# Layer 0's columns behind an up scan: their loads on GpSimd's queue instead of ScalarE's

## The chip, the cores and the metric

The kernel runs on one core of one Trainium2 chip. The metric is the device time of one execution in microseconds (us); lower is better. A core has a matrix engine (TensorE, PE in the profile; PEld is its weight load), a vector engine (VectorE, DVE), a scalar engine (ScalarE, ACT), a general engine (GpSimd, POOL) and SyncE (SP), which only issues DMA transfers. ScalarE and GpSimd can issue transfers as well. Each engine works through its own instructions in order, and all transfers are carried out by the core's 16 DMA engines.

## The reference

The input x has the shape (32, 48, 64, 128): batch, channels, height, width. Two layers are computed, each as x = x + scan(groupnorm(x)). A scan goes over the image four times: down and up over the 64 rows, with one set of weights, then right and left over the 128 columns. Each step adds a convolution of the row (or column) before it, with five taps along the row (or column) and 48 x 48 channels:

```python
def step(w, b):
    def f(carry, inp):
        nxt = inp + _conv1d(carry, w, b)
        return (nxt, nxt)
    return f
...
_, d_rest = jax.lax.scan(step(down_w, down_b), d0, xs[1:])
...
_, u_rest = jax.lax.scan(step(down_w, down_b), u0, seq)
...
_, r_rest = jax.lax.scan(step(right_w, right_b), r0, ws[1:])
...
_, l_rest = jax.lax.scan(step(left_w, left_b), l0, R[Ww - 2::-1])
...
x = x + _L0_conv_ref(_gn(x), L0_conv_down_w, ...)
x = x + _L1_conv_ref(_gn(x), L1_conv_down_w, ...)
```

So a column scan can't begin before the up scan of the same images has ended: column 0 holds an element of every row.

## The kernel before

The batch is cut into four groups of 8 images. `PHASES` (line 75) lists the work in the order in which TensorE does it: a "rows" phase is the down and up scan of one group (126 steps), a "cols" phase is the right and left scan of a pair of groups (254 steps). For layer 0 the order is rows of groups 0 and 1, columns of pair 0, rows of group 2, rows of group 0 of layer 1, rows of group 3, columns of pair 1. Each of the two column phases of layer 0 thus follows directly on the rows of its pair's second group; `follows` (line 800) is true for these two phases alone.

A step (`step`, line 647) makes nine matrix products, three for each third of the 384 channel places, and a VectorE add (L667) for each third, which takes the product from PSUM and one tensor from SBUF. Three large slots of the `arena` hold the rows or columns that are worked on.

Rows and columns have different layouts in SBUF, and the data goes from one to the other by way of a DRAM tensor, `upa` for layer 0. `move_rows` (line 517) stores rows of the up scan there as they are finished; with `to_dram` it makes ten transfers for eight rows, one for each entry of `PIECES`. `load_unit` (line 561) loads columns from there, also in up to ten transfers for one run over the three thirds. The 128 columns are taken in four quarters j of 32; a quarter has six units i, a third (o) of one group of the pair (half). Units with half = 1 belong to the group whose up scan has just ended. Within a unit `a` counts eight runs of eight rows (a = 0 is rows 0-7), and `e` is the row inside the run. All transfers go through `dma` (L199), which uses SyncE's queue if it isn't given another.

When something is issued is written out by hand. `at(t, ...)` (line 737) puts a call on an agenda, t in scan steps; `catch_up` (line 1072) makes the calls that are due before each step, and `in_order` (line 203) keeps the instructions of each engine in that order. t0 is the step at which a phase begins. The last rows of an up scan are stored at these times: the cut [2, 8) when row 2 is done, the cut [0, 2) at the end (`plan_rows`, line 770). `plan_cols` (line 805) loads quarter 0 of the group just scanned in five calls that follow the stores: runs 4-7, 2-3, 1, then rows 2-7, then rows 0-1. Quarter 1 comes at t0 + 1.5, quarter 2 from t0 + 8.

```python
at(t0 + 1.5, load_unit, k, 1, i, 0, NH, 0, E8, nc.scalar)
...
at(t0 + (38 if after else 8) + 2 * i, load_unit, k, 2, i)
```

The first goes to ScalarE's queue, behind the calls for quarter 0; the second to SyncE's.

In the built program each transfer tells of its landing by a semaphore. SyncE's and ScalarE's transfers share eight of these in turn, and a transfer waits until the one that had its semaphore before has landed. Transfers issued from GpSimd have eight others.

Of the kernel before, what the change touches and what calls it, by code (L numbers as in the profile page):

```python
# [91 lines left out]
def kernel(  # L92
# [8 lines left out]
    nc = tc.nc  # L101
# [456 lines left out]
    def quarter(k, j):  # L558
        return slot[slots(k)[j % 3]].rearrange("p (o s n) -> p s o n", s=2, o=NG)
# [177 lines left out]
    def at(t, fn, *args):  # L737
        agenda.append((t, len(agenda), fn, args))

    def spread(t, gen, every):  # L740


        def go(t):
            if next(gen, "end") != "end":
                at(t + every, go, t + every)
                agenda.sort(key=lambda a: a[:2])

        at(t, go, t)
# [51 lines left out]
    def follows(k):  # L800

        _, layer, pair = PHASES[k]
        return PHASES[k - 1] == ("rows", layer, 2 * pair + 1)

    def plan_cols(k, t0, prev):
        _, layer, pair = PHASES[k]
        n = 2 * NG
        after = prev == "cols"
        for i in range(n):
            if follows(k) and UNITS[i][1] == 1:  # L810
                other = nc.scalar
                at(t0 - 31 + i, load_unit, k, 0, i, 4, NH, 0, E8, other)
                at(t0 - 13 + i, load_unit, k, 0, i, 2, 4, 0, E8, other)
                at(t0 - 6 + i / n, load_unit, k, 0, i, 1, 2, 0, E8, other)
                at(t0 - 1.5, load_unit, k, 0, i, 0, 1, E8 // 4, E8, other)
                at(t0, load_unit, k, 0, i, 0, 1, 0, E8 // 4, other)
            else:
                early = 30 if after else 46 if k == 2 else 70
                at(t0 - early + 2 * i, load_unit, k, 0, i)
            if follows(k):  # L820

                at(t0 + 1.5, load_unit, k, 1, i, 0, NH, 0, E8, nc.scalar)
            else:
                at(t0 + (3 if after else -24 + 2 * i), load_unit, k, 1, i)
            at(t0 + (38 if after else 8) + 2 * i, load_unit, k, 2, i)
            at(t0 + 33 + 2 * i, spill_unit, k, i, False)
            at(t0 + 50 + 2 * i, load_unit, k, 3, i)
        final = k == len(PHASES) - 1
        left = t0 + W - 1
        end = left + W - 1  # L830
        for i in range(n):

            t = left + 64 + 2 * i if layer == 0 else left + 39.5 + 4.5 * i
            at(t, spill_unit, k, i, True)
        units = []
        for n_done, j in enumerate((3, 2, 1, 0)):
            every = 4.5
            if j == 0 and PHASES[k + 1 if not final else k][0] == "rows":
                every = 7
            units += [(left + 34 + 32 * n_done + every * i, j, i) for i in range(n)]  # L840
        stats = None
        if layer == 0:
            stats = ResultStatsV(f"r{2 * pair}"), ResultStatsA(f"r{2 * pair + 1}")
        tiles = [stage[:, i] for i in range(4)]
        if layer:
            tiles += spare_tiles[0 : 2 if final else 1]
        n = len(tiles)
        direct = [u for u in units if not (final and u[1] == 0)]

        for u, (t, j, i) in enumerate(direct):  # L850
            nat = tiles[u % n]
            o, half = UNITS[i]
            if u < n:
                at(left + 16, load_residual, k, j, i, nat)
            if layer == 0:
                if u >= n:
                    at(direct[u - n][0] + 3, load_residual, k, j, i, nat)
                at(t, add_residual, k, j, i, nat)
                at(t + 4, keep_result, k, j, i)
                unit = quarter(k, j)[:, half, o]  # L860
                if half == 0:
                    for b in range(GB):
                        at(t + 5 + b, stats[0].take, j, o, unit, b)
                else:
                    at(t + 1, stats[1].take, j, o, unit)
            else:

                at(t, add_residual, k, j, i, nat)
                at(t + 2.5, permute_unit, k, j, i, nat, (nc.gpsimd, nc.scalar, nc.scalar))
                if final or j not in HELD:  # L870
                    at(t + 4.5, store_result, k, j, i, nat)
                else:
                    at(t + 4.5, hold_result, j, i, nat)
                if final and j == 1:
                    at(t + 4.7, load_residual, k, 0, i, last_tiles(k)[i])

                if u >= 2 and u - 2 + n < len(direct):
                    at(t + 4.6, load_residual, k, *direct[u - 2 + n][1:], tiles[(u - 2) % n])
        if layer == 0:
            t = units[-1][0] + 14  # L880
            g = 2 * pair
            spread(t, scaling(f"r{g}", 1, g, stats[0], r_masks), 1)
            spread(t + 20, scaling(f"r{g + 1}", 1, g + 1, stats[1], r_masks), 1)
        if layer:

            at(left + 10, nc.scalar.copy, junk[:, BN - 1 :], quarter(k, 3)[:, 0, 0, RUN - 1 : RUN])
        if layer and not final:
            todo = [(j, half, e) for j in HELD for half in range(2) for e in range(E8)]
            for n, what in enumerate(todo):
                at(end + 63 + 1.9 * n, let_result, *what)  # L890
        if final:
            at(end + 4, last_results, k)

    def last_tiles(k):

        s = slot[slots(k)[2]].rearrange("p (i n) -> p i n", i=2 * NG)
        return [s[:, i] for i in range(2 * NG)]
# [13 lines left out]
    for k, (kind, layer, _) in enumerate(PHASES):  # L911
        (plan_rows if kind == "rows" else plan_cols)(k, starts[k], PHASES[k - 1][0])
# [223 lines left out]
```

## Time and profile before

| | |
|---|---|
| median of 3 runs | 4380.13 us (4379.56 to 4392.25) |
| the profiled execution | 4375.56 us, of which the span on the page is 4373.8 us |
| mean granted TensorE clock | 0.98 |
| TensorE idle before the first right scan of layer 0 | 22.6 us, until a load from `upa` |
| TensorE idle before the second | 20.1 us, until a load from `upa` |
| loads from `upa` on ScalarE's queue | 120, 60 in each column phase of layer 0 |
| DMA engines busy in the first idle time (661.20 to 683.45) | 0.85, at 156 GB/s |

The page gives for each engine its busy time and the number of instructions; then groups of instructions with their busy time, mean length and the idle time before them, with what ended it. A queue of transfers is written with a q (SPq, ACTq). The names step_01u and step_00r mean: layer 0, group 1, up scan; layer 0, pair 0, right scan. Busy time of a transfer's row is the time its engine took to issue it, not the time it took to land.

### The profile page before, as it was taken

Reading aid. Unit: us, or ns where it says so; the run is one execution under the profiler, and the core shown is the slowest. Engines: PE = TensorE matmul, PEld = TensorE weight load, DVE = VectorE, ACT = ScalarE, POOL = GpSimd, SP = SyncE. Lnnn points to the kernel's source line nnn. Section 1 sums busy time; section 2 is a strip of 40 time slices with the busy share of each in tenths; the row PEclk is TensorE's granted clock in tenths of the full one; section 3 lists DMA queues with packets and bytes.
Section 4 is the critical chain, followed back from the end, with each engine's and each line's share of the span. In section 5 each row is a group of like instructions: output and inputs, shape, how many; then the busy total and the mean of one; then the engine's idle time right before and its main releaser. Section 6 shows DMA issues by size and latency. Waiting matters only on the chain. (4 is left out here: it accounts for less than half of the span.)

```text
span 4373.8 us, 90099 instructions
## 1 busy us (share of the span) xinstructions
PE 4149.4 (95%) x36632; PEld 4120.7 (94%) x36632; DVE 2164.2 (49%) x6558; ACT 1360.7 (31%) x2698; POOL 820.4 (19%) x775
## 2 busy tenths in 40 slices
PE   5889997999999999998999999999999999999992
PEld 2889997999999999998999999999999999999992
DVE  6344443456665444443446665444444444444443
ACT  2783301434785554100005774503000002110122
POOL 4351000324332020000004310000000024510352
PEclk9999998999999999999999999999999999999996
DMA  9989789866999989579407989939188039989999
GB/s 194 176 171 154 116 149 183 225 120 189 235 195 147 155 156 158 99 124 209 77 1 222 224 174 143 134 51 165 35 141 189 1 76 240 245 239 159 168 196 182
DMA packets 2111167, 680.34 MB, mean 156 GB/s; under 512 B 2000928, under 2 KB 2053920, under 8 KB 2070816
## 3 DMA queue, kind: packets, MB, share of 16 engines
q1 hardware_dynamic: 2010496, 576.00, 69.7%
q10 hardware_dynamic: 100256, 98.59, 10.8%
q8 instruction: 288, 4.72, 0.5%
q14 instruction: 127, 1.04, 0.1%
HBM read 397.57 MB, written 295.98 MB: 159 GB/s over the span
## 5 line engine op out<-in xcount | busy, mean ns | idle before, releaser
L542 ACT ACTIVATE arena<-arena,offset,scale 128x256 f32<-128x256 f32 (+2 forms) x864 | 601.2, 790 | 412.4 <-DVE arena L667 142.4
L595 POOL TENSOR_TENSOR arena<-arena 128x2048 f32<-128x2048 f32 x80 | 363.0, 4553 | 1660.0 <-PE step_01l L658 504.4
L499 POOL COPY arena<-arena 112x256 f32<-112x256 f32 x458 | 270.3, 646 | 753.7 <-DMA arena<-in_x 504.1
L433 ACT ACTIVATE early<-arena 128x256 f32<-128x256 f32 x192 | 129.5, 675 | 687.5 <-DMA arena<-xin 547.4
L658 PE MATMUL step_00r<-arena,early 128*128 128x128 f32 x2286 | 258.6, 277 | 22.6 <-DMA arena<-upa 22.6
L658 PEld LDWEIGHTS step_00r<-arena,early 128*128 128x128 f32 x2286 | 258.4, 194 | 22.9 <-issue 22.8
L658 PE MATMUL step_01r<-arena,early 128*128 128x128 f32 x2286 | 257.4, 276 | 20.1 <-DMA arena<-upa 20.1
L658 PEld LDWEIGHTS step_01r<-arena,early 128*128 128x128 f32 x2286 | 257.1, 193 | 20.4 <-issue 20.3
L364 ACT ACTIVATE early<-arena 112x512 f32<-112x512 f32 x192 | 121.0, 630 | 460.5 <-PE step_00r L658 246.6
L658 PE MATMUL step_11r<-arena,early 128*128 128x128 f32 x2286 | 258.9, 277 | 3.9 <-DVE arena L667 3.9
L658 PEld LDWEIGHTS step_11r<-arena,early 128*128 128x128 f32 x2286 | 258.2, 193 | 4.4 <-DVE arena L667 4.2
L658 PE MATMUL step_00l<-arena,wleft 128*128 128x128 f32 x2286 | 256.3, 275 | 0.0
L658 PE MATMUL step_10r<-arena,early 128*128 128x128 f32 x2286 | 256.0, 275 | 0.0
L658 PEld LDWEIGHTS step_10r<-arena,early 128*128 128x128 f32 x2286 | 255.7, 192 | 0.3
L658 PEld LDWEIGHTS step_00l<-arena,wleft 128*128 128x128 f32 x2286 | 255.7, 192 | 0.0
L658 PE MATMUL step_11l<-arena,wleft 128*128 128x128 f32 x2286 | 255.5, 275 | 0.0
L658 PE MATMUL step_10l<-arena,wleft 128*128 128x128 f32 x2286 | 255.5, 275 | 0.0
L658 PE MATMUL step_01l<-arena,wleft 128*128 128x128 f32 x2286 | 255.4, 275 | 0.0
L658 PEld LDWEIGHTS step_10l<-arena,wleft 128*128 128x128 f32 x2286 | 255.4, 192 | 0.0
L658 PEld LDWEIGHTS step_11l<-arena,wleft 128*128 128x128 f32 x2286 | 255.4, 192 | 0.0
L658 PEld LDWEIGHTS step_01l<-arena,wleft 128*128 128x128 f32 x2286 | 255.3, 192 | 0.0
L620 ACT COPY arena<-arena 128x256 f32<-128x256 f32 x172 | 99.5, 657 | 415.5 <-POOL arena L595 127.5
(175 smaller groups left out, 7043.9 us busy)
## 6 DMA issues: line engine op xcount, KB each, us to landing
xin<-arena SPq DMA_DIRECT2D x96, 384.0 KB, 5.5
arena<-xin SPq DMA_DIRECT2D x96, 384.0 KB, 8.1
mid<-arena SPq DMA_DIRECT2D x96, 384.0 KB, 7.8
arena<-mid SPq DMA_DIRECT2D x192, 192.0 KB, 4.4
upb<-arena SPq DMA_DIRECT2D x192, 192.0 KB, 3.9
arena<-upb SPq DMA_DIRECT2D x96, 384.0 KB, 11.8
arena<-xin SPq DMA_DIRECT2D x186, 192.0 KB, 4.3
upa<-arena SPq DMA_DIRECT2D x180, 192.0 KB, 3.9
```

The costliest lines, as they stand in the source:

```text
L364: nc.scalar.activation(junk[0:P], piece, AF.Identity, accum_out=self.sum[:, at[0], at[1]],)
L433: nc.scalar.activation(junk[:, 0:n], view[:, b], AF.Identity, accum_out=self.sum[:, i, j : j + 1])
L499: copy(dst[:, r, q], src[:, r0 + r, q])
L542: nc.scalar.activation(args[0], args[0], AF.Identity, bias=args[2], scale=args[1])
L595: eng.tensor_tensor(unit, unit, nat, ALU.add)
L620: copy(by_w(perm)[:, a], src[:, a])
L658: nc.tensor.matmul(part(whole(ps[o]), -s), weights[:, i, FULL * (o - NG * s - i + 1) : FULL * (o - NG * s - i + 2)], part(src(i), s), star ...
```

## The change

In the five calls of `plan_cols` that load quarter 0 for the group just scanned, the queue is GpSimd's instead of ScalarE's. Nothing else differs: the times on the agenda, the transfers' sizes and all other queues are as they were. Quarter 1's loads stay on ScalarE's queue.

```diff
@@ -808,7 +808,7 @@
         after = prev == "cols"
         for i in range(n):
             if follows(k) and UNITS[i][1] == 1:
-                other = nc.scalar
+                other = nc.gpsimd
                 at(t0 - 31 + i, load_unit, k, 0, i, 4, NH, 0, E8, other)
                 at(t0 - 13 + i, load_unit, k, 0, i, 2, 4, 0, E8, other)
                 at(t0 - 6 + i / n, load_unit, k, 0, i, 1, 2, 0, E8, other)
                 at(t0 - 1.5, load_unit, k, 0, i, 0, 1, E8 // 4, E8, other)
                 at(t0, load_unit, k, 0, i, 0, 1, 0, E8 // 4, other)
```

In the built order 40 transfers in each of the two column phases of layer 0 stand on GpSimd's queue instead of ScalarE's: ten each for runs 4-7, 2-3 and 1, eight for rows 2-7 and two for rows 0-1. GpSimd's own instruction ahead of the first ones is its copy of an up scan's first row (L208), and the next after them are copies (L499) of the input of another group or adds (L595). On the other engines the order of the instructions doesn't change, apart from the semaphores that they wait for.

## The prediction

> **What bounds the kernel now.** I read the page's totals first, then the groups for what ended the matmuls' idle time, then who waits for the `upa` loads, then the timeline and the transfers around that wait.
>
> ```profile
> PE 4149.4 (95%) x36632; PEld 4120.7 (94%) x36632; DVE 2164.2 (49%) x6558; ACT 1360.7 (31%) x2698; POOL 820.4 (19%) x775
> L658 PE MATMUL step_00r<-arena,early 128*128 128x128 f32 x2286 | 258.6, 277 | 22.6 <-DMA arena<-upa 22.6
> L658 PE MATMUL step_01r<-arena,early 128*128 128x128 f32 x2286 | 257.4, 276 | 20.1 <-DMA arena<-upa 20.1
> ```
>
> TensorE is busy 95% of the span: a serial chain of scan steps. The change can only reach the two gaps where a right scan of layer 0 waits for its columns, 42.7 us together, so 1.0% of the time is the most there is. The rest of each line is matmul time that doesn't change.
>
> How the first gap (660.8 to 683.45) is spent:
>
> ```profile
> 660.85 0.35 DVE L667 SCALAR_TENSOR_TENSOR arena<-step_01u,bd,early 128x128 f32<-128x128 f32 x1 [0.22 <-PE step_01u L658]
> 659.26 2.20 ACTq L199 DMA_DIRECT2D arena<-upa  x5
> 661.46 6.52 SPq L199 DMA_DIRECT2D upa<-arena  x9
> 668.03 6.39 SPq L199 DMA_DIRECT2D upa<-arena  x9
> 670.26 3.62 ACTq L199 DMA_DIRECT2D arena<-upa  x8
> 674.52 1.62 SPq L199 DMA_DIRECT2D arena<-upa  x3
> 676.17 0.78 ACTq L199 DMA_DIRECT2D arena<-upa  x2
> arena<-upa SPq DMA_DIRECT2D x2, 384.0 KB, 5.5
> arena<-upa SPq DMA_DIRECT2D x1, 256.0 KB, 6.8
> arena<-upa ACTq DMA_DIRECT2D x2, 48.0 KB, 6.8
> 683.45 16.80 PE L658 MATMUL step_00r<-arena,early 128*128 128x128 f32 x122 [22.63 <-DMA arena<-upa]
> ```
>
> The columns are start and length in us, then engine, line and operation; the three rows without a start give a count, KB each and the median us from issue to landing. (A count can be one or two short where a query's window cuts the row.) The last row is finished on VectorE at 661.2. SP stores rows 2-7 from 661.46 and rows 0-1 until 674.4, landing at 675.9. ScalarE's queue then issues its last two loads at 676.17; they land 6.8 us later, where loads of 48 KB at 670-674 took 2.0, because SP's three loads for quarter 2 (1 MB, issued 674.52-676.1) went ahead of them. The second gap is alike: VectorE ends at 1966.76, the last two loads are issued at 1979.36, land 6.5 us later, and TensorE starts at 1986.49.
>
> **What the Trainium skill says.** (1) "DMA: Bandwidth & Descriptors", Specifications: the first byte takes about 1 us on GpSimd's path, where software writes the descriptors, and about 0.6 us on the SP/ACT path. The trace has no GpSimd DMA; ScalarE's issues take 0.43-0.45 us each. (2) Same page, "Issuing engines are not separate DMA queues": all run on the same 16 engines, and another queue saves issue time only. The 2.0 against 6.8 us above agrees. (3) Same page, "Queues, rings and completion order": an engine takes turns between queues packet by packet. Between SP and ScalarE the trace looks more like order of arrival. For GpSimd's queue no run shows it. (4) "SBUF — State Buffer", "Who interferes with whom": VectorE blocks GpSimd's port only in 2-port modes or with two SBUF inputs. The step's add reads PSUM and one SBUF tensor, and VectorE is idle in the gap, so I charge nothing.
>
> **The change part by part.** At each of the two places 40 loads (ten each for runs 4-7, 2-3 and 1, then eight and two for run 0) leave ScalarE's queue for GpSimd's.
>
> *Removed: waits by shared semaphores.* In the built order SP's and ScalarE's DMAs share eight completion semaphores in turn, and each waits for the DMA that had its semaphore before. So SP's stores wait for ScalarE's loads, which wait for earlier stores. The store of 644.60 is followed by one at 648.03, and rows 2-7, whose row 2 was finished at about 657.2, begin at 661.46. GpSimd's loads have semaphores of their own, so SP's stores follow only each other. Worked out:
> - Rows 8-15: from 644.25 at the pace of the chunk before (ten issued 628.2-636.6, 8.4 us) to 652.7, landing about 4 us later (4.1 in the trace): 656.5, where ScalarE was released at 659.26.
> - Rows 2-7: from 656.5 for 6.9 us to 663.4, landed 666.
> - Rows 0-1: 6.4 us before, with three waits for ScalarE's loads in it; I take 5, to 668.4, landed 670.5, against 675.9. At the second place the same, 1305.56 us later (VectorE ends at 1966.76 there and at 661.20 here).
>
> *Added: GpSimd's issue.* Let T be one issue. GpSimd's queue is in order and nothing of its own stands ahead (its copy at 534.68 is long done, its next work starts at 710.74, and the 40 loads end before that). Ten loads start at 656.5, eight at the later of 666 and 656.5+10T, two at the later of 670.5 and the end of those. Lower bound for T: 0.43, ScalarE's own. Upper: 2.0, the whole fixed cost of a GpSimd DMA on that page ("Anatomy of one DMA"). I take 1.4, an estimate: the 1 us that the page gives to software descriptors plus the measured 0.43. Then GpSimd is the late one: 656.5 + 20 x 1.4 = 684.5 for the last issue, 14 us after the stores have landed.
>
> *Moved: quarter 1's loads.* ScalarE's 20 loads for quarter 1 stood behind the 40; now three (1 MB, of the older group) go at about 605-610, where the engines have slack later (0.57 busy at 640-650), so nothing. The other 17 go when the stores have landed, 670.5, no longer behind the critical loads, and SP's loads for quarter 2 and of `in_x` from 668.4. So the loads that TensorE needs share the engines with about 2.9 MB (1 + 0.77 + 1.1). Landing L: below 2.0 (alone), above 12.9 (ScalarE's 384 KB issued at 682.9-684 behind both queues). I take 6.8, measured behind one such queue.
>
> *Sum.* First place: 684.5 + 6.8 = 691.3 against 683.45: +7.9. Second: 691.3 + 1305.56 = 1996.9 against 1986.49: +10.4. Together +18.3. What is released earlier on ScalarE and SP is needed only at column 32, 64 us later, and gives nothing. The profiled execution took 4375.56 (span 4373.8), so 4393.9; the median shown is 4.6 above it, so 4398.
>
> **Rivals.**
> - *No visible change.* With T near 1.0 the earlier stores pay for the slower issue: 656.5 + 20 + L of 2 to 6.8 gives 678.5 to 683.3, so -5.0 to -0.2 and at the second place -2.4 to +2.3; together -7 to +2, 4373 to 4382. For it: the page's 1 us may already hold all of an issue. Against: T has to hit a narrow window, as the break-even is 20T + L = 27.0 and 24.4.
> - *Faster.* If T is at most 0.6 and GpSimd's queue gets its turn, the last two are issued at 670.5 to 671.4 and land in 1.9-3: 673.3 to 675, -8 to -10 and -5.5 to -7.6: about -16, 4364. The floor, with T 0.43, is -17.8, 4362. For it: the stores do come 5 us earlier. Against: software is priced above hardware.
> - *Contention, on the slow side too:* T near 1, but each small descriptor waits for 8 KB ones of two other queues, for the eight as for the two: L 13 gives 689.5, +6 and +8.6, and more if the eight pile up: 4395 to 4420. Worst corner, T 2.0 and L 12.9: 709.4, +26 and +28.5, 4435.
> - *That it doesn't move:* the built order shows 80 loads gone from ScalarE and 80 on GpSimd, with matmuls and SP's order unchanged; excluded.
>
> **How the numbers follow.** The bound for telling a change is 0.3%, 13 us: 4367 and 4393. Slower, by issue or contention: 0.47. No visible change: 0.35. Faster: 0.18. The likeliest is slower, 4398, its own range 4393 to 4424. Since other cases hold half, the range reaches from 4365 (all but the floor of the faster case) to 4424 (short of the worst corner).
>
> **What would show it.** Right: matmuls of step_00r and step_01r idle about 30 us each for `arena<-upa`, now issued by POOL; POOL's issues of these stand back to back through the gap, starting before 660; SP's last stores end near 668 and 1974. Wrong: if POOL's last two issues follow the last store at once, T is under 0.7 and it is faster. If SP's stores end no earlier, the semaphores weren't what delayed them, and it is slower by some 10 us more. If POOL is in time but its loads land late, contention is the cause.

## The result, and the profile after

The changed kernel takes 4389.69 us (median of 14 runs, 4386.36 to 4393.58), the kernel before beside it 4380.44 (14 runs, 4377.23 to 4392.25). The ratio is 1.0018, with a 95% interval of 1.0010 to 1.0026: slower by some 4 to 11 us. Built and run a second time, beside other kernels, it gave 1.0017 (1.0009 to 1.0025).

The page after, totals, DMA queues and groups, answers to the lines shown of before:

```profile
PE 4150.1 (94%) x36632; PEld 4121.1 (94%) x36632; DVE 2167.7 (49%) x6558; ACT 1360.4 (31%) x2698; POOL 861.5 (20%) x855
...
q0 software_dynamic: 3200, 6.30, 0.6%
...
L658 PE MATMUL step_01r<-arena,early 128*128 128x128 f32 x2286 | 257.1, 276 | 25.4 <-DMA arena<-upa 25.4
L658 PE MATMUL step_00r<-arena,early 128*128 128x128 f32 x2286 | 257.3, 276 | 24.9 <-DMA arena<-upa 24.9
```

POOL has 80 instructions more (855 against 775). q0 is a queue that the kernel before did not use: packets, megabytes, share of the 16 engines. The gap before step_00r went from 22.6 to 24.9 us and the one before step_01r from 20.1 to 25.4. Together +7.6 us, and what ends them is still a load from `upa`.

The profiled execution of after was the slowest of its kernel, 4393.58, so the two traces differ by 18 us, more than the medians do. Of that, 7.6 are the two gaps. The first scan step starts at 106.5 us instead of 94.8, and a wait inside step_11r, a scan of layer 1, grew from 3.9 to 9.5; the first row scans together, and the end of the program, are some 3 us shorter. The edit touches none of these places. Over all traces of this study the wait in step_11r is 3.0 to 9.5, with no order by kernel. The first step starts between 94.8 and 107.7, and here the three kernels with nothing on GpSimd's queue are the three earliest (94.8, 97.6 and 100.4; the ten other traces have 100.5 to 107.7). Whether that queue has a part in the start was not tried. At the start of the last scan before the first gap the two sets overlap (534.0 to 537.0 and 534.7 to 542.7), and the table at the end of the experiments comes within 2 us of every measured interval without it. In the second trace of the changed kernel both gaps are 24.9; of the kernel before there is one trace.

The timeline of after at the first place (start and length in us, engine, line, operation, count, and in brackets the idle time before):

```profile
666.47 11.96 SPq L199 DMA_DIRECT2D upa<-arena  x18
...
668.21 4.95 POOL L199 DMA_DIRECT2D arena<-upa  x10 [9.56 <-DMA upa<-arena]
...
669.53 0.35 DVE L667 SCALAR_TENSOR_TENSOR arena<-step_01u,bd,early 128x128 f32<-128x128 f32 x1 [0.22 <-PE step_01u L658]
676.55 5.05 POOL L199 DMA_DIRECT2D arena<-upa  x10 [3.40 <-DMA upa<-arena]
678.53 1.34 SPq L199 DMA_DIRECT2D arena<-upa  x3
679.92 12.40 SPq L199 DMA_DIRECT2D arena<-in_x  x2
680.15 17.72 ACTq L199 DMA_DIRECT2D arena<-upa  x9
...
694.39 5.86 PE L658 MATMUL step_00r<-arena,early 128*128 128x128 f32 x36 [24.90 <-DMA arena<-upa]
```

Three things are to be seen. GpSimd issues quickly: ten loads in 4.95 us. It is not the late one: it stands idle for 3.40 us until a store has landed. And the stores come earlier: SP's last one is issued by 678.43, 8.6 us after VectorE's end at 669.9, where it took 13.2 before. It landed at 680.0 (10.1 us after VectorE's end; 14.7 before), and GpSimd's last two loads went out at 680.60 and 681.10. Up to there about 4 us are won. But the last two landed at 692.27 and 693.59, 12 us later, where the same loads took 6.8 before. In those 12 us SP's three loads for quarter 2 and one of `in_x`, issued from 678.53, and ScalarE's loads for quarter 1, let go by the same last store at 680.15, move as well. The view by windows (length; busy us and instructions of each engine; clock; busy share of the DMA engines; GB/s):

```profile
680.00:694.40 14.40, 0.01 (x1) 0.04 (x1) 0.00 (x0) 0.00 (x0) 1.50 (x4) 0.50 1.01 203
```

The DMA engines are full over the whole wait. Added up by queue over this window from the trace's packets, SP's queue moved 1522 KB, ScalarE's 1155 KB and GpSimd's 246 KB, the last in packets of at most 3072 bytes that stand scattered among the others' of 2048 and 8192. At 203 GB/s GpSimd's bytes alone are 1.2 us of work.

Counted from VectorE's end, the last load is issued 4.1 us earlier than before (11.2 against 15.3), takes 5.7 longer to land (12.5 against 6.8), and TensorE starts 0.8 after it instead of 0.1: +2.3 us. At the second place it is issued 0.4 earlier (12.6 against 13.0), takes 5.5 longer (11.9 against 6.4), and TensorE starts 0.2 later after it: +5.3.

### The profile page after: what moved, and what is told of

The parts are those of the page before. It is cut to its first block, busy times and chain, and to the rows that moved or that the text cites. A ratio compares the mean times of both kernels' runs of the same rounds, so it can differ in the third digit from the quotient of the medians.

```text
span 4391.7 us, 90191 instructions
## 1 busy us (share of the span) xinstructions
PE 4150.1 (94%) x36632; PEld 4121.1 (94%) x36632; DVE 2167.7 (49%) x6558; ACT 1360.4 (31%) x2698; POOL 861.5 (20%) x855
## 5 line engine op out<-in xcount | busy, mean ns | idle before, releaser
L595 POOL TENSOR_TENSOR arena<-arena 128x2048 f32<-128x2048 f32 x80 | 362.9, 4554 | 1534.4 <-PE step_10l L658 450.1
L499 POOL COPY arena<-arena 112x256 f32<-112x256 f32 x458 | 270.4, 647 | 604.4 <-DMA arena<-in_x 358.3
L658 PE MATMUL step_01r<-arena,early 128*128 128x128 f32 x2286 | 257.1, 276 | 25.4 <-DMA arena<-upa 25.4
L658 PE MATMUL step_00r<-arena,early 128*128 128x128 f32 x2286 | 257.3, 276 | 24.9 <-DMA arena<-upa 24.9
L658 PEld LDWEIGHTS step_11r<-arena,early 128*128 128x128 f32 x2286 | 258.8, 194 | 10.1 <-DVE arena L667 9.9
## 6 DMA issues: line engine op xcount, KB each, us to landing
arena<-upb SPq DMA_DIRECT2D x96, 384.0 KB, 11.9
```

The costliest lines, as they stand in the source:

```text
L499: copy(dst[:, r, q], src[:, r0 + r, q])
L595: eng.tensor_tensor(unit, unit, nat, ALU.add)
L658: nc.tensor.matmul(part(whole(ps[o]), -s), weights[:, i, FULL * (o - NG * s - i + 1) : FULL * (o - NG * s - i + 2)], part(src(i), s), star ...
```

## The experiments

Theory A, from the two traces: two effects work against each other. GpSimd's loads no longer take semaphores from SP's stores, so the stores land earlier; but the last ten loads, formerly ahead of ScalarE's loads for quarter 1, now share the DMA engines with those and with SP's. The first effect can be seen in before's trace, in what SP's queue waited for from 644 to 676 us (total, number of waits, longest):

```profile
SPq L199 <- DMA arena<-upa: 7.3, 6, 3.4
```

In after, from 652 to 679, it waits for no load from `upa`. Theory A's rivals are named anew in each expectation, so theory B of the first three experiments is not that of the later ones. "Hold" means a small instruction that reads one column of quarter 0 (or of quarter 1), so that it waits for the loads there, put on an engine ahead of the loads that are to wait. All kernels compute the whole reference; in those with a hold on SP the lines stand two further down.

### Quarter 1 held back

In the changed kernel, a copy on ScalarE ahead of quarter 1's loads:

```diff
+        if follows(k):
+            at(t0 + 1.3, nc.scalar.copy, junk[:, BN - 1 :], quarter(k, 0)[:, 1, 0, 0:1])
```

> The change, with ScalarE's 20 loads of quarter 1 held back: a copy of one element of column 0 stands ahead of them, so they start when the critical loads have landed. Theory A (the critical loads land late because two other queues start at the same moment and GpSimd's queue gets one packet a turn): one of the two rivals is gone, so the last two loads land 6 to 8 us after issue instead of 12, TensorE's gap before the right scan is 18 to 20 us instead of 25, the time about 4379. Theory B (a load issued from GpSimd is slow in itself, whatever the traffic): the gap stays at 25, the time at 4390.

Measured: ratio 1.0011 (1.0003 to 1.0019), gaps of 21.8 and 21.2 us:

```profile
L658 PE MATMUL step_00r<-arena,early 128*128 128x128 f32 x2286 | 258.4, 277 | 21.8 <-DMA arena<-in_x 21.8
L658 PE MATMUL step_01r<-arena,early 128*128 128x128 f32 x2286 | 258.0, 276 | 21.2 <-DMA arena<-upa 21.2
```

(The name of a load of `in_x` in the first line is inferred by the profile and can't be right: that load landed at 688.84, after the scan had started at 687.91. The last load from `upa` landed 0.8 us before the start.) The last two loads took 8.8 to 9.5 us to land instead of 12, which is more than the 6 to 8 of theory A. Without quarter 1's stream the waits are 3 and 4 us shorter.

### SP's loads held back

In the changed kernel, a store of one column to a new DRAM tensor on SP's queue, ahead of quarter 2's loads:

```diff
+    holder = dram.tile([FULL, 1], F32, tag="holder", name="holder")
...
+        if follows(k):
+            at(t0 + 1.4, dma, holder, quarter(k, 0)[:, 1, 0, 0:1])
```

> The change, with SyncE's loads of quarter 2 and of the input held back until the critical loads have landed (a store of one element of column 0 per partition stands ahead of them); ScalarE's quarter 1 is not held. Theory A: the last two loads land 6 to 8 us after issue, the gap is 18 to 20 us, the time about 4379. If SyncE's traffic is the larger part of the delay, less than that, and more than e1_hold_act gains. Theory B: gap 25, time 4390.

Measured: ratio 1.0001 (0.9993 to 1.0010), gaps of 20.4 and 19.8:

```profile
L660 PE MATMUL step_01r<-arena,early 128*128 128x128 f32 x2286 | 258.5, 277 | 19.8 <-DMA arena<-upa 19.8
L660 PE MATMUL step_00r<-arena,early 128*128 128x128 f32 x2286 | 257.6, 276 | 20.4 <-DMA arena<-upa 20.4
```

The last load landed 8.0 and 7.5 us after its issue, the one before it 5.9 and 5.6. Against quarter 1's loads alone GpSimd's are late as well.

### Both held back

The two instructions above, in one kernel:

> The change, with both queues held back until the critical loads have landed. Theory A: the last two loads land 2 to 3 us after issue, the gap is about 14 us at both places, the time 4390 - 2 x 11 = 4368, so also below the kernel before. Theory B: gap 25, time 4390.

Measured: ratio 1.0006 (0.9997 to 1.0014). Both gaps are as theory A has them, 14.3 and 14.4, and the loads land within 2 us. With nothing beside it, GpSimd's queue is no slower than ScalarE's was when alone (2.0 in the kernel before), so theory B, that such a load is slow in itself, is out. Of the 10 us between 12 and 2, holding one stream takes away 3 or 4 and holding both takes away all: either stream by itself keeps most of the delay. But the time is not shorter. The timeline of this kernel, at the first gap and at column 32, shows why:

```profile
676.90 53.28 PE L660 MATMUL step_00r<-arena,early 128*128 128x128 f32 x462 [14.28 <-DMA arena<-upa]
...
746.64 5.14 SPq L201 DMA_DIRECT2D arena<-upa  x5
...
754.55 0.35 DVE L669 SCALAR_TENSOR_TENSOR arena<-step_00r,bd,arena 128x128 f32<-128x128 f32 x1 [11.85 <-DMA arena<-upa]
754.96 2.21 PEld L660 LDWEIGHTS step_00r<-arena,early 128*128 128x128 f32 x10 [11.34 <-DVE arena L669]
754.96 2.29 PE L660 MATMUL step_00r<-arena,early 128*128 128x112 f32 x9 [11.15 <-DMA arena<-upa]
```

The add of column 32 waits 11.85 us for a load from `upa`. It is the last of quarter 1's, which was issued on ScalarE's queue at 741.89 and landed at 754.34. Quarter 1 was let go at the same moment as SP's loads of quarter 2 and `in_x`, stood among them, and came 11 us after the scan, which had started early, needed it. Part of this is not traffic: ScalarE issued nothing from 703.6 to 720.0, because the next of its loads, at 720.03, had the semaphore of a load of `in_x` on SP's queue, which landed at 719.96. (In the kernel before the same kind of wait lasts from 695.4 to 710.7.) How much of the lateness is traffic and how much is such waits was not separated. The second place has no wait at column 32. A transfer held back comes due later: the next limit of these phases is quarter 1, 66 us after the start of the scan. In the kernel before, its last load landed at 749.95, with the scan at that column at about the same time (683.45 + 66), so there was no slack for an earlier start.

### The kernel before, SP's loads held back

The same store on SP's queue in the kernel before, with nothing on GpSimd's queue:

> The kernel before (critical loads on ScalarE's queue), with SyncE's loads of quarter 2 and of the input held back as in e2_hold_sp. If the 6.8 us that its last two loads took came from SyncE's traffic, they land about 2 us after issue: gaps of 18 and 15.7 us instead of 22.6 and 20.1, the time 4380 - 9 = 4371. If 6.8 us is what such a load takes at that place, the gaps stay.

Measured: ratio 0.9982 (0.9971 to 0.9993), faster than before. The groups:

```profile
L660 PE MATMUL step_01r<-arena,early 128*128 128x128 f32 x2286 | 258.6, 277 | 16.3 <-DMA arena<-upa 16.3
L660 PE MATMUL step_00r<-arena,early 128*128 128x128 f32 x2286 | 257.1, 276 | 17.4 <-DMA arena<-upa 17.4
```

The stores are as late as before (14.5 and 13.3 us after VectorE's end), but the last two loads land in 1.7 to 1.8 us. On ScalarE's queue they stand ahead of quarter 1 by their order, so one hold is enough. This is what SP's traffic costs in the kernel before: 9 us in two gaps.

### The last ten loads back on ScalarE's queue

The thirty earlier loads per place stay on GpSimd's queue:

```diff
-                at(t0 - 1.5, load_unit, k, 0, i, 0, 1, E8 // 4, E8, other)
-                at(t0, load_unit, k, 0, i, 0, 1, 0, E8 // 4, other)
+                at(t0 - 1.5, load_unit, k, 0, i, 0, 1, E8 // 4, E8, nc.scalar)
+                at(t0, load_unit, k, 0, i, 0, 1, 0, E8 // 4, nc.scalar)
```

> The changed kernel, with the last ten loads per place (rows 2-7 and rows 0-1 of the columns) back on ScalarE's queue, ahead of quarter 1's; the thirty earlier ones stay on GpSimd's. Theory A (two separate effects: GpSimd's loads free SP's stores, and a GpSimd load is served by turns against the other two queues): stores land about as early as in the changed kernel (10 to 12 us after VectorE's last add), the last two loads are issued right after and, on a hardware queue, stand behind SP's 1 MB of quarter 2 alone: 5.5 to 7 us to land, gaps of 17 to 19 us at both places, 6 to 10 us less than before, about 4368. Theory B (it is only the amount of data in flight that makes the loads late, whichever queue they are on): the loads take 9 us as with quarter 1 held back alone, gaps of 20 to 22 us, no change from before. Theory C (the stores are late because ScalarE's last ten loads share their semaphores, not because of the thirty earlier ones): stores land 14 to 15 us after VectorE, gaps of 21 to 23.

Measured: ratio 0.9999 (0.9990 to 1.0007), gaps of 20.3 and 20.2. None of the three theories has this as it stands: the gaps are those of theory B, by which only the amount of data in flight counts, but the landing time is A's, 6.6 us. The stores land 12.2 and 12.6 us after VectorE's end, between A (10 to 12) and C (14 to 15). At the first place 2.5 us of the stores' delay went with the thirty loads and some 2 stayed with the last ten; at the second nothing went.

### Only the last ten on GpSimd's queue

The reverse, from the kernel before:

> The kernel before, with only the last ten loads per place on GpSimd's queue. Theory A: the stores stay late (13 to 15 us after VectorE's last add), and the last two loads take about 12 us to land by GpSimd's queue: gaps of 26 to 28 us at both places, 10 to 13 us more than before, about 4388. Theory B: quarter 2 and quarter 1 stand against them as in the changed kernel, landing about 12 too, so the gap is the same 26 to 28. Theory C: the stores come as early as in the changed kernel, gaps of 24 to 25.

Measured: ratio 1.0058 (1.0044 to 1.0071), about 25 us slower, twice what theory A had. The timeline at the first place:

```profile
668.86 33.42 ACTq L199 DMA_DIRECT2D arena<-upa  x17
669.11 0.35 DVE L667 SCALAR_TENSOR_TENSOR arena<-step_01u,bd,early 128x128 f32<-128x128 f32 x1 [0.22 <-PE step_01u L658]
669.44 16.41 SPq L199 DMA_DIRECT2D upa<-arena  x18
684.13 5.19 POOL L199 DMA_DIRECT2D arena<-upa  x10 [140.69 <-DMA upa<-arena]
685.95 1.36 SPq L199 DMA_DIRECT2D arena<-upa  x3
...
702.36 2.05 PE L658 MATMUL step_00r<-arena,early 128*128 128x128 f32 x8 [33.29 <-DMA arena<-upa]
```

The loads' part came as expected: the last two took 10.7 to 13.4 us. The stores' part did not: they landed 18.3 and 17.7 us after VectorE's end, later than in either kernel. With the last ten gone from ScalarE's queue, three of quarter 1's loads, which belong to the older group and need no store, were issued at 672.44 to 673.26, right behind the run of rows 8-15. SP's stores of rows 2-7, issued at 672.74 and 673.09, took 6.5 and 7.7 us to land beside them, where the stores of these rows took 2.3 to 3.7 us in the kernel before. So, as the trace has it (it was not tried by itself), what keeps quarter 1 back before is the place of these ten loads on ScalarE's queue. In the changed kernel the same three loads go at 614 to 616, well ahead of these stores.

### The last ten back, and SP's loads held back

> As with the last ten loads back on ScalarE's queue, and a store of one column of quarter 0 on SP's queue ahead of quarter 2's loads, so that these wait for the loads that TensorE needs. Theory A: stores 10 to 12 us after VectorE, loads landing in 2 to 3 us: gaps of 13 to 15 us at both places, some 13 us less than before, if quarter 1 (column 32, 66 us later) is in time; in the kernel before its last load lands only about when it is needed, so at the first place up to 8 us can come back as a wait there: about 4360 to 4368. Theory B: the same. Theory C: stores at 14 to 15, gaps of 17 to 18 as in the kernel before with the same hold, about 4367.

Measured: ratio 0.9998 (0.9988 to 1.0008). The page puts two waits into each scan:

```profile
L660 PE MATMUL step_00r<-arena,early 128*128 128x128 f32 x2286 | 260.4, 278 | 21.4 <-DMA arena<-upa 16.2
L660 PE MATMUL step_01r<-arena,early 128*128 128x128 f32 x2286 | 260.0, 278 | 20.0 <-DMA arena<-upa 14.4
```

The gaps are 16.2 and 14.4; the rest, 5.3 and 5.6 us, are waits inside the scans. They are the add of column 32 again, here at both places. The gain of 12 us in the gaps came back almost whole as waits for quarter 1.

### The hold moved to quarter 1: three kernels

If quarter 1 is late because SP's loads are let go beside it, then a hold that lets SP go only when part of quarter 1 has landed must take the wait away. It replaces the hold on quarter 0 on SP's queue:

```diff
+        if follows(k):
+            at(t0 + 1.6, dma, holder, quarter(k, 1)[:, 0, 1, 0:1])
```

With the last ten loads back on ScalarE's queue:

> The last ten loads per place back on ScalarE's queue, and SP's hold moved later: the store on SP's queue ahead of quarter 2's loads now reads a column of quarter 1 (its third unit), so SP's loads of quarter 2 and of in_x wait until part of quarter 1 has landed too. Theory A (in the version with the hold on quarter 0 the 11 us of waits at column 32 are quarter 1's loads, slowed by SP's that were let go with them): gaps of 14 to 17 us at both places, no wait of over 1 us inside step_00r and step_01r, about 12 us less than before, ratio 0.997. Rival (quarter 1 is late because of its own 20 loads' semaphores and start, not because of SP's): the waits inside the two scans stay at 5 to 6 us each, no change from before.

In the kernel before:

> The kernel before, with the same later hold on SP's queue: nothing on GpSimd's queue. Theory A: stores at 13 to 15 us after VectorE's last add, loads landing in 2 us, gaps of 16 to 17.5 us as with the hold on quarter 0 (17.4 and 16.3), quarter 1 earlier than there and so no wait at column 32: 9 us less than before, ratio 0.998; the thirty loads on GpSimd's queue are then worth 2 to 3 us. Rival: holding SP's queue longer delays in_x and quarter 2 until something later waits: less gain than with the hold on quarter 0, or none.

In the changed kernel, with ScalarE's hold on quarter 0 as in the first experiment:

> The changed kernel (all forty loads on GpSimd's queue), with ScalarE's hold on quarter 0 ahead of quarter 1's loads and SP's later hold on quarter 1. Theory A: as with both holds on quarter 0, nothing stands against the loads that TensorE needs: they land in 2 us and the gaps are 14.3 us at both places; and quarter 1, no longer against SP's loads, is in time: no wait at column 32, so 14 us less than before, ratio 0.997. Rival: quarter 1 starts too late for column 32 whatever SP does: 8 to 11 us come back inside step_00r, no change from before.

Measured: 0.9973 (0.9963 to 0.9983), 0.9985 (0.9978 to 0.9991) and 0.9967 (0.9953 to 0.9980). The last has the lowest ratio of the study, though its interval overlaps that of the first: 4362.85 us where the kernel before took 4376.78 on that chip. Its first gap, and its groups:

```profile
673.76 3.94 POOL L201 DMA_DIRECT2D arena<-upa  x8 [4.05 <-DMA upa<-arena]
678.52 1.00 POOL L201 DMA_DIRECT2D arena<-upa  x2 [0.82 <-DMA upa<-arena]
681.10 0.19 ACT L210 COPY early<-arena 128x1 f32<-128x1 f32 x1 [183.33 <-DMA arena<-upa]
681.51 2.82 ACTq L201 DMA_DIRECT2D arena<-upa  x6
...
681.78 2.45 PE L660 MATMUL step_00r<-arena,early 128*128 128x128 f32 x10 [14.23 <-DMA arena<-upa]
```

```profile
L660 PE MATMUL step_01r<-arena,early 128*128 128x128 f32 x2286 | 257.8, 276 | 13.8 <-DMA arena<-upa 13.8
L660 PE MATMUL step_00r<-arena,early 128*128 128x128 f32 x2286 | 257.4, 276 | 14.2 <-DMA arena<-upa 14.2
```

The loads issued at 678.52 and 679.0 land by 681.0; ScalarE's loads begin only at 681.51; and the idle time is the gap alone, so quarter 1 is in time (its last load landed at 738.71, where the scan was due there at about 748). With the loads protected, what the queue does for the stores can be read: they land 10.0 and 9.7 us after VectorE's end, against 13.9 and 12.0 in the kernel before with the same later hold, and TensorE's idle time is 28.0 us against 32.1. So GpSimd's queue is worth some 4 us here, together with ScalarE's hold, which stands in for the order that the loads had on ScalarE's queue. The intervals of these two kernels overlap at their ends, so that 4 rests on the traces.

### The changed kernel again, and all runs in one table

> The changed kernel once more, for a second trace and beside the others on the same chip: gaps of 24 to 26 us at both places if these are its own; the stretch before the first step, which took 11 us longer in its first trace, between 95 and 107 us as in all the other traces; 6 to 11 us more than before.

Measured: 1.0017 (1.0009 to 1.0025), gaps of 24.9 and 24.9.

TensorE's idle time in step_00r and step_01r, from each page, set against the measured ratio in us (ratio less 1, times 4380):

| kernel | idle, both | less 42.7 | measured, 95% |
|---|---|---|---|
| changed kernel | 50.3 | +7.6 | +4 to +11 |
| changed kernel again | 49.8 | +7.1 | +4 to +11 |
| + quarter 1 held | 43.0 | +0.3 | +1 to +8 |
| + SP held | 40.2 | -2.5 | -3 to +4 |
| + both held | 39.8 | -2.9 | -1 to +6 |
| before + SP held | 33.7 | -9.0 | -13 to -3 |
| last ten back | 41.0 | -1.7 | -4 to +3 |
| only last ten on GpSimd's | 64.3 | +21.6 | +19 to +31 |
| last ten back + SP held | 41.4 | -1.3 | -5 to +4 |
| last ten back + hold on quarter 1 | 29.5 | -13.2 | -16 to -7 |
| before + hold on quarter 1 | 32.1 | -10.6 | -10 to -4 |
| changed + hold on ScalarE and on quarter 1 | 28.0 | -14.7 | -21 to -9 |

Nine of twelve lie in their interval; the other three miss it by 1 to 2 us. Each row, and the 42.7 of the kernel before, rests on one trace. The two gaps, with the waits at column 32, carry the result.

## Why the prediction was right or wrong

- *Only the two gaps can change*: right as far as the table shows; whether the start of the program changes too is open, as said with the result.
- *Removed: waits by shared semaphores.* Right in kind, and 1 to 2 us short in size: the last store was put at 9.3 us after VectorE's end, and landed at 10.1 and 11.3 (10.7 and 10.6 in the second trace), where it took 14.7 and 12.5 before; so the second place won only 1 to 2 us. That it depends on what ScalarE's queue shares with SP's is shown from both sides: with all forty loads on GpSimd's queue 9.7 to 11.3 in every kernel; with all on ScalarE's 12.0 to 14.7; with the last ten on ScalarE's 11.3 to 12.6. That semaphores are what they share was read from the built order and from the waits of SP's queue shown above; no experiment changed the semaphores alone.
- *Added: GpSimd's issue.* This step failed. T, the time of one issue, was taken as 1.4 us, the Trainium skill's 1 us for software descriptors ("DMA: Bandwidth & Descriptors", Specifications) plus ScalarE's 0.43. One issue takes 0.50 us (median of 80), near the lower bound. The forecast had GpSimd as the late one, its last issue ending 23.3 us after VectorE's end; it ended at 11.7. The page's figure is for the first byte, and was added where it did not belong: ten issues follow each other at 0.50 us, so 1 us of it can't be in the queue's pace.
- *Landing L*, from the last issue to the landing. Failed too, the other way. It was taken at 6.8, "measured behind one such queue", and measured at 12, next to the upper bound of 12.9. The prediction counted the 2.9 MB that would share the engines, and then priced one stream. In the experiments it is 9.4 without quarter 1's stream, 8 without SP's and 2 without both.
- *Sum.* For the first place: 30.1 us from VectorE's end to TensorE's start were predicted. T takes 11.6 off, L adds 5.2, and 0.8 more pass between the recorded landing and the first matmul: 24.5, as measured. Two errors of opposite sign gave the right direction; that it came out right was luck. With T of 0.50 and L of 6.8 the same working gives 678.3 and 1983.9, some 5 and 3 us earlier than before.
- *Contention*, the rival on the slow side, has the mechanism, though with T near 1. Its "more if the eight pile up" came too: of the eight loads of rows 2-7 at the first place the last four took 5.1 to 10.8 us to land, where before none took more than 2.3. The page "DMA: Bandwidth & Descriptors", Queues, rings and completion order, has an engine take turns between queues packet by packet; the packets of after agree with that roughly. From ScalarE's first packet of 8192 bytes to GpSimd's last, the queues of GpSimd, SP and ScalarE moved 112, 213 and 126 packets at the first place (7.4 us) and 64, 62 and 99 at the second (6.6 us), those of 4 bytes included. In number they are within a factor of two, while of the bytes GpSimd moved a ninth and a twelfth. The exact rule of turns was not measured. Nor was it tried to put quarter 1's loads on GpSimd's queue too, behind the forty, which would keep the old order there.
- *Faster* named T of at most 0.6 and a landing in 1.9 to 3 us as its conditions. The first holds. The second holds only in kernels with holds; there the change comes out on that side. (Its -5.5 for the second place should be -5.9: 675 and 1305.56 make 1980.56, against 1986.49.)
- *What would show it*: "if POOL's last two issues follow the last store at once, T is under 0.7 and it is faster" was a wrong test, since it took the landing for granted. "If POOL is in time but its loads land late, contention is the cause" is what came.
- *Size.* 4398 was forecast, 17.9 above the median; the measured difference is about 8. The time lies in the range. By size it is the case of no visible change, inside 0.3%, which was given 0.35; by mechanism it is contention.

## What to carry to other kernels

When a load is moved to another queue, ask what stood behind it on the old one: the order on a queue was a priority, and whatever is let go by the same event becomes its rival. Where queues share semaphores, look also for a load on one queue that stops another until it has landed. Price the landing with all the bytes that start at the same moment, not with the one stream that was there before. When a wait is shortened by holding other transfers back, look up when those come due: here quarter 1 took the gain back until SP's loads were held behind it.

## What the runs showed of the hardware

- An issue on GpSimd's queue took 0.50 us (median; 0.49 to 0.72), almost ScalarE's 0.43 to 0.45, and with nothing beside it a 48 KB load by it landed in about 2 us, as by ScalarE's.
- Against full queues of SP and ScalarE, the same load landed in 12 us, although GpSimd's bytes were a twelfth of what the engines moved in 14.4 us of the wait (246 of 2923 KB). In number of packets GpSimd's queue was not behind to that degree (64 against 62 and 99 at the second place).
- Three of SP's stores of rows 2-7 took 6.5 to 7.7 us beside three large loads on ScalarE's queue; in the kernel before these rows' stores took 2.3 to 3.7.
